# Another order of the eight groups of score products on TensorE's array tiles

## The chip, the cores and the metric

The kernel runs on one core of one Trainium2 chip. The metric is device time in microseconds of one execution. The engines are TensorE (PE, with its weight loads listed apart as PEld), VectorE (DVE), ScalarE (ACT), GpSimd (POOL) and SyncE (SP), which here issues nearly all DMAs. Each engine runs its own list of instructions in the order in which the program gives them, and engines wait for each other through semaphores.

## The reference

A cross-attention block with a feed-forward part, in float32: 128 sequences of 128 tokens, width 256, 16 heads of 16, hidden width 1024.

```python
q = (query @ Wq + bq).reshape(b, s, N_HEADS, D_K).transpose(0, 2, 1, 3)
k = (key @ Wk + bk).reshape(b, s, N_HEADS, D_K).transpose(0, 2, 1, 3)
v = (values @ Wv + bv).reshape(b, s, N_HEADS, D_K).transpose(0, 2, 1, 3)
scores = jnp.einsum('bhqd,bhkd->bhqk', q, k) / jnp.sqrt(jnp.float32(D_K))
allowed = j < i + mask
scores = jnp.where(allowed, scores, NEG_INF)
attn = jax.nn.softmax(scores, axis=-1)
...
ctx = ctx.transpose(0, 2, 1, 3).reshape(b, s, d)
attn_out = ctx @ Wo + bo
x = layer_norm(query + attn_out, ln1_g, ln1_b)
ffn = jax.nn.relu(x @ W1 + b1) @ W2 + b2
out = layer_norm(x + ffn, ln2_g, ln2_b)
```

With mask 0 a token attends only to the tokens before it, so the first 64 queries need only the first 64 keys.

## The kernel before

The 128 sequences are worked on as 64 pairs, numbered 0 to 63. Weights stay in SBUF. The kernel is a software pipeline written out by hand: in the regular step of pair p (pairs 9 to 60, `step`, a loop over the list `ORDER`) PE computes the scores and values of pair p, the queries and keys of p+1, the output projection of p-2, the first feed-forward product of p-4 or p-3 and the second of p-5 or p-4, and so on. The same operations stand one by one in a long list for the pairs ahead of 9 and behind 60. Nothing is reordered by a scheduler: each engine gets its instructions as the list names them, and the framework adds the semaphore waits.

PSUM is one tile, `banks`, of eight banks, which the operations share by hand. The change concerns `scores_both` (its matmul is L440), which is called for every pair from 4 on, in the regular step between `context` and `res0`:

- The queries qT and keys kT lie in SBUF with 32 rows for a group of heads, so there are four **strips** of 32 rows, r = 0 to 3. The 128x128 array of PE is used as eight tiles of 32 rows and 64 columns: the strip r gives the rows, the sequence s of the pair (0 or 1) the columns.
- Each strip has products for two values of m, and for two halves of the queries: `hi` = 0 is the first 64 queries, a **narrow** product of 128 columns, and `hi` = 1 the second 64 queries, a **wide** product of 256 columns. That gives 4 x 2 x 2 x 2 = 32 products, each left in the profile as two records.
- A wide product of strip r goes to bank r, a narrow one to bank 4 + r.
- `scores_both` issues them as eight groups of four: the strips 0 and 1 (`one`) or 2 and 3 (`two`), one half, one m, and in each group s outside and r inside.

Around it, within one step: `weigh` (L586, L596) multiplies the probabilities of pair p-2 with its values into bank 7, and DVE reads that bank in `context` (L612, then L617 twice). ACT reads banks 0 and 1 in `relu_even` (L1399, called re1 to re3). After the scores PE goes on with `v1`, the first value products (L1147). DVE then masks the narrow scores (L464 for banks 4 and 5, L456 for banks 6 and 7) and the wide ones (L1552, bank by bank, beginning with bank 3, then 1, 2 and 0, the last three behind `low_maximum`, L920). The keys reach kT through a DMA (`ks`, `ks2`, "kT<-kr"). `turnx` (L1614) is a transpose on DVE ahead of `context`.

```python
        weigh addbo re0-2 vr-1 hf-2 re2-2 re1-2 turnx-1 xc2-1 re3-2 context scores res0 ro3-2
        ro0-2 br1 maskA0 ro2-2 add3 oc0 ro1-2 v1 maskA1 oc2 maskB hs0-1 o1 max3 vk1 vk0 q1
```

Of the kernel before, what the change touches and what calls it, by code (L numbers as in the profile page):

```python
# [19 lines left out]
def tile_cross_attention_block(  # L20
# [165 lines left out]
    one = const.tile([1, P], F32, tag="one", name="one")  # L186
# [61 lines left out]
    def at_bank(i, name):  # L248
        return banks[:, i]
# [141 lines left out]
    def room(p, hi):  # L391

        st = states[p]
        if "sm" not in st:
            st["sm"] = wide(f"sm_{p}") if p != 1 else turned_all
        at = H * P if not hi else 0
        n = P if hi else HP
        st["sm", hi] = st["sm"][:, at : at + H * n].rearrange("p (h j) -> p h j", j=n)
        st["nmx", hi] = small.tile([P, H], F32, tag=f"nmx{hi}", name=f"nmx{hi}_{p}")
# [22 lines left out]
    def scores_both(p):  # L422

        st = states[p]
        st["both"] = True
        for hi in range(2):
            st["sps", hi] = [
                at_bank(r if hi else 4 + r, f"pss{hi}_{p}_{r}") for r in range(NS)
            ]
            room(p, hi)  # L430
        one, two = (0, 1), (2, 3)
        for strips, hi, m in (
            (one, 0, 0), (two, 1, 0), (one, 0, 1), (two, 1, 1),
            (one, 1, 0), (one, 1, 1), (two, 0, 0), (two, 0, 1),
        ):
            n = P if hi else HP
            for s in range(2):
                for r in strips:
                    strip, first = slice(32 * r, 32 * r + 32), s * P
                    nc.tensor.matmul(  # L440
                        st["sps", hi][r][
                            s * HP : (s + 1) * HP, m * 2 * n : (m + 1) * 2 * n
                        ].rearrange("p (e j) -> p e j", e=2),
                        st["qT"][strip, m, first + hi * HP : first + hi * HP + HP],
                        st["kT"][strip, m, :, first : first + n],
                        start=True, stop=True,
                    )
# [1190 lines left out]
    def bring_part(p, n):  # L1638
# [3 lines left out]
    OPS = {  # L1642
        "weigh": lambda p: weigh(p - 2),
        "scores": lambda p: scores_both(p),
        "context": lambda p: context(p - 2),
        "deviations": lambda p: scales_of(p),
# [381 lines left out]
    tokens(5, "c")  # L2028
    bring(3, nc.sync, LATE_FIRST[7:])
    scores_both(4)  # L2030
    mask(4, 0, A)
    mask(4, 1, A)
# [31 lines left out]
    spread_values(4)  # L2064
    stack_values(4)
    scores_both(5)
    tokens(6, "c")
    mask_high(5, 2, 2)
# [1024 lines left out]
```

## Time and profile before

| What | us |
|---|---|
| median of three runs | 1478.88 |
| lowest and highest run | 1476.47, 1479.12 |
| span of the profiled execution, first to last instruction | 1476.0 |
| PE busy in it | 1450.0 |
| one regular step (pair 33 to pair 34) | 22.03 |
| score products, L440, of pair 33, from the first to the first product behind them | 1.60 |

No time of the profiled execution other than its span is listed, so the span stands for it, 0.47 us below the lowest run. In the rows of the profile a timeline entry gives start, duration, engine, line, operation and the tiles written and read, and how many instructions were merged; the duration of merged PE rows runs to the modelled end of the last one, so successive rows overlap. Rows of windows give the stretch, its length, and the busy time of each engine with the number of its instructions that ran in it: PE first, then PEld; the rows of a quarter to a tenth of a microsecond and shorter are restricted to L440.

### The profile page before, as it was taken

The numbers are of one execution on the slowest core, as the hardware profiler recorded it, in microseconds if no ns is written. First come the engines' busy times: TensorE is split into PE (matmuls) and PEld (weight loads), VectorE is DVE, ScalarE is ACT, GpSimd is POOL, SyncE is SP. The second block draws the span as 40 slices with busy tenths as digits, with TensorE's granted clock in tenths as the row PEclk, the third lists the DMA queues.
The fourth block names the chain that finished last, engine by engine and source line by source line (L and its number), as shares of the span: only waits on it lengthen the run. The fifth ranks groups of instructions, "written<-read, shape, count | busy, mean of one in ns | idle before, by whom it ended". The sixth has DMA issues, their size and how long they took to land.

```text
span 1476.0 us, 61938 instructions
## 1 busy us (share of the span) xinstructions
PE 1450.0 (98%) x20713; PEld 1394.3 (94%) x20713; DVE 1372.8 (93%) x3231; ACT 1304.3 (88%) x5559; POOL 1266.4 (86%) x1816
## 2 busy tenths in 40 slices
PE   8999899999999999999999999999999999999998
PEld 7778799999999999999999999999999999999988
DVE  6987999999999999999999999999999999999767
ACT  4659899999999999999999999999999999999743
POOL 5986898988988988988988988888898888887966
PEclk9999999999999999999999999999999999999999
DMA  8274766766766767776766766766776766774541
GB/s 202 66 142 104 178 162 149 159 152 156 167 158 155 154 152 157 169 159 152 165 147 151 166 157 157 163 149 153 163 160 157 161 147 154 163 163 113 130 109 51
DMA packets 367448, 220.33 MB, mean 149 GB/s; under 512 B 279600, under 2 KB 335152, under 8 KB 367152
## 3 DMA queue, kind: packets, MB, share of 16 engines
q1 hardware_dynamic: 364864, 214.27, 63.9%
q8 instruction: 187, 3.06, 0.9%
q10 hardware_dynamic: 2288, 2.11, 0.7%
q14 instruction: 109, 0.89, 0.2%
HBM read 55.06 MB, written 18.09 MB: 50 GB/s over the span
## 4 chain that ended last, share of the span: by engine, by line
PE 72%; ACT 7%; DVE 4%; DMA 3%; SPq 1%; POOL 1%; issue 1%; DVEq 0%; ACTq 0%; POOLq 0%
PE banks L1147 40%; PE banks L1358 20%; PE banks L440 5%; ACT sm L931 5%; PE banks L596 3%; DMA kT<-kr 2%; PE banks L586 2%; PE banks L971 1%; DMA brought<-turned 1%; ACT kr L1213 1%; PE banks L869 0%; PE banks L1044 0%; ACT qT L1175 0%; SPq L552 0%; PE banks L629 0%
## 5 line engine op out<-in xcount | busy, mean ns | idle before, releaser
L931 ACT ACTIVATE sm<-banks,nmx 128x128 f32<-128x128 f32 x944 | 336.8, 383 | 15.8 <-DVE nmx L1558 12.6
L931 ACT ACTIVATE sm<-sm,nmx 128x64 f32<-128x64 f32 x944 | 321.6, 369 | 1.4 <-DVE nmx L920 1.4
L533 DVE STREAM_TRANSPOSE turned<-sm 128x1024 f32<-128x1024 f32 x186 | 217.0, 1213 | 3.3 <-DMA brought<-turned 2.4
L931 ACT ACTIVATION_READ_ACCUMULATOR sm<-banks,nmx 128x1 f32 x944 | 211.4, 224 | 0.0
L931 ACT ACTIVATION_READ_ACCUMULATOR sm<-sm,nmx 128x1 f32 x944 | 207.8, 220 | 0.0
L1147 PE MATMUL banks<-wt,hS 128*128 128x128 f32 x1344 | 177.6, 275 | 0.0
L1358 PE MATMUL banks<-xS,w1t 128*128 128x128 f32 x1344 | 177.2, 275 | 0.0
L1147 PEld LDWEIGHTS banks<-wt,hS 128*128 128x128 f32 x1344 | 163.6, 192 | 0.1
L1358 PEld LDWEIGHTS banks<-xS,w1t 128*128 128x128 f32 x1344 | 163.4, 192 | 0.0
L1558 DVE TENSOR_REDUCE nmx<-banks 128x4 f32<-128x512 f32 x224 | 152.1, 679 | 1.9
L1547 POOL TENSOR_TENSOR hS<-hT 128x512 f32<-128x512 f32 x116 | 147.5, 1273 | 5.4 <-ACT hT L876 2.4
L1358 PE MATMUL banks<-brought,w 128*128 128x128 f32 x896 | 118.2, 275 | 0.0
L1608 POOL TENSOR_TENSOR x1b<-x,g_r 128x512 f32<-128x512 f32 x56 | 72.3, 1291 | 51.0 <-ACT x L703 51.0
L1147 PE MATMUL banks<-w,hT 128*128 128x128 f32 x896 | 109.8, 275 | 0.0
L1358 PEld LDWEIGHTS banks<-brought,w 128*128 128x128 f32 x896 | 109.0, 192 | 0.0
L440 PE MATMUL banks<-kT,qT 32*64 32x128 f32 (+1 forms) x3840 | 100.7, 331 | 6.3 <-DMA kT<-kr 3.7
L1147 PEld LDWEIGHTS banks<-w,hT 128*128 128x128 f32 x896 | 104.8, 192 | 0.1
L440 PEld LDWEIGHTS banks<-kT,qT 32*64 32x64 f32 x3840 | 82.7, 131 | 16.9 <-ACT hT L1399 4.9
L1534 POOL TENSOR_TENSOR oc<-cxT 128x128 f32<-128x128 f32 x112 | 49.0, 457 | 57.9 <-DVE cxT L617 56.9
L1387 ACT ACTIVATE hT<-hT,b1e_c 128x256 f32<-128x256 f32 x224 | 95.7, 509 | 1.2 <-DVE hT L1383 1.1
L1552 DVE TENSOR_TENSOR banks<-banks,neg 128x256 f32<-128x256 f32 x224 | 93.1, 416 | 0.0
L703 ACT ACTIVATE x<-t,nb,sd 128x256 f32<-128x256 f32 x126 | 68.4, 592 | 19.1 <-POOL nb L726 11.9
(322 smaller groups left out, 4841.1 us busy)
## 6 DMA issues: line engine op xcount, KB each, us to landing
brought<-turned SPq DMA_DIRECT2D x936, 128.0 KB, 2.4
out_dram<-t SPq DMA_DIRECT2D x63, 256.0 KB, 4.7
xb<-in_x_dram SPq DMA_DIRECT2D x124, 128.0 KB, 3.2
cb<-in_ctx_dram SPq DMA_DIRECT2D x124, 128.0 KB, 3.2
x<-in_x_dram SPq DMA_DIRECT2D x31, 512.0 KB, 5.4
kT<-kr SPq DMA_DIRECT2D x112, 128.0 KB, 2.7
brought<-turned SPq DMA_DIRECT2D x40, 96.0 KB, 2.2
w<-in_L_xattn_W_dram SPq DMA_DIRECT2D x2, 1024.0 KB, 7.8
```

Of the source, the lines that this page charges most:

```text
L440: nc.tensor.matmul(st["sps", hi][r][s * HP : (s + 1) * HP, m * 2 * n : (m + 1) * 2 * n].rearrange("p (e j) -> p e j", e=2), st["qT"][strip ...
L533: nc.vector.transpose(turned[:, :, at : at + 256].rearrange("p j (n a) -> p n j a", a=32), states[p]["sm", hi].rearrange("p h j -> p (h j) ...
L703: nc.scalar.activation(x1[:, s], t1[:, s], AF.Identity, bias=st["nb", 1][:, s], scale=sd[:, s])
L931: nc.scalar.activation(sm[:, h, :], src, AF.Exp, bias=nmx[:, h : h + 1], scale=1.0, **({"accum_out": st["su"][:, at : at + 1]} if summed e ...
L1147: nc.tensor.matmul(out, left(k) if self.depth > 1 else left, right(k) if self.depth > 1 else right, start=(n == 1 and k == 0), stop=(k == ...
L1358: nc.tensor.matmul(ps[:, i * P : (i + 1) * P].rearrange("p (n a) -> p n a", a=32), left(i), right, start=(n in (1, 2, 5) and i == 0), stop ...
L1387: nc.scalar.activation(self.hT[:, f, at], self.hT[:, f, at] if src is None else src, AF.Relu, bias=b1e_c[:, f : f + 1], scale=1.0,)
L1534: nc.gpsimd.tensor_tensor(c[:, n], left, right, how)
L1547: engine.tensor_tensor(c[:, n], left, right, how)
L1552: nc.vector.tensor_tensor(ps[:, :, HP:], ps[:, :, HP:], neg[:, 1, None, :].to_broadcast([P, 4, HP]), ALU.add)
L1558: nc.vector.tensor_reduce(states[p]["nmx", 1][:, 4 * b : 4 * b + 4], banks[:, b].rearrange("p (n j) -> p n j", j=P), AX.X, ALU.max, negate ...
L1608: nc.gpsimd.tensor_tensor(st["x1b"], st["x1b"] if n else st["x1"], (be1b_r if n else g1_r)[:, None, :].to_broadcast([P, 2, D]), ALU.add if ...
```

## The change

Of the eight groups in `scores_both`, two change places with the next one. The fourth group, the wide one of strips 2 and 3 with m = 1, goes behind the wide one of strips 0 and 1 with m = 0. The wide one of strips 0 and 1 with m = 1 goes behind the narrow one of strips 2 and 3 with m = 0.

```diff
         for strips, hi, m in (
-            (one, 0, 0), (two, 1, 0), (one, 0, 1), (two, 1, 1),
-            (one, 1, 0), (one, 1, 1), (two, 0, 0), (two, 0, 1),
+            (one, 0, 0), (two, 1, 0), (one, 0, 1), (one, 1, 0),
+            (two, 1, 1), (two, 0, 0), (one, 1, 1), (two, 0, 1),
         ):
```

On each strip the order of its own products is the same as before: narrow, narrow, wide, wide on strips 0 and 1, and wide, wide, narrow, narrow on strips 2 and 3. The first place is PE in pair 10, from the end of `weigh` to `v1`, before the change. The size is that of the output: 64x128 is a narrow product, 64x256 a wide one; kT and qT are the keys and queries of this pair.

```order
L596 MATMUL banks<-brought,vz_174 32x64 x16
L440 MATMUL banks<-kT_170,qT_3025 64x128 [waits DMAHW5_49,DMAHW4_49,Activation_49]
L440 MATMUL banks<-kT_170,qT_3025 64x128 x3
L440 MATMUL banks<-kT_170,qT_3025 64x256 [waits DVE_49]
L440 MATMUL banks<-kT_170,qT_3025 64x256 x3
L440 MATMUL banks<-kT_170,qT_3025 64x128 x4
L440 MATMUL banks<-kT_170,qT_3025 64x256 x4
L440 MATMUL banks<-kT_170,qT_3025 64x256 [waits Activation_49]
L440 MATMUL banks<-kT_170,qT_3025 64x256 x7
L440 MATMUL banks<-kT_170,qT_3025 64x128
L440 MATMUL banks<-kT_170,qT_3025 64x128 [waits DVE_49]
L440 MATMUL banks<-kT_170,qT_3025 64x128 x6
```

And the same place after the change:

```order
L440 MATMUL banks<-kT_170,qT_3025 64x256 [waits DVE_49]
L440 MATMUL banks<-kT_170,qT_3025 64x256 x3
L440 MATMUL banks<-kT_170,qT_3025 64x128 x4
L440 MATMUL banks<-kT_170,qT_3025 64x256 [waits Activation_49]
L440 MATMUL banks<-kT_170,qT_3025 64x256 x7
L440 MATMUL banks<-kT_170,qT_3025 64x128
L440 MATMUL banks<-kT_170,qT_3025 64x128 [waits DVE_49]
L440 MATMUL banks<-kT_170,qT_3025 64x128 x2
L440 MATMUL banks<-kT_170,qT_3025 64x256 x4
L440 MATMUL banks<-kT_170,qT_3025 64x128 x4
L1147 MATMUL banks<-wv,cT_3063 128x128 [waits DVE_49]
```

The product that waits for ACT, into bank 0, was the 17th of the 32 and is the 13th. The second narrow product of strips 2 and 3, into bank 7, which waits for DVE, was the 26th and is the 22nd; four wide products of strips 0 and 1 that stood ahead of it stand behind it now.

The second place is PE in pair 6, one of the pairs ahead of the regular step, before the change. Here the third group, narrow on strips 0 and 1, waits for ACT in its first product:

```order
L440 MATMUL banks<-kT_170,qT_1648 64x128 [waits Activation_49]
L440 MATMUL banks<-kT_170,qT_1648 64x128 [waits DVE_49]
L440 MATMUL banks<-kT_170,qT_1648 64x128 x2
L440 MATMUL banks<-kT_170,qT_1648 64x256 x4
L440 MATMUL banks<-kT_170,qT_1648 64x128 [waits Activation_49]
L440 MATMUL banks<-kT_170,qT_1648 64x128 x3
L440 MATMUL banks<-kT_170,qT_1648 64x256 x5
L440 MATMUL banks<-kT_170,qT_1648 64x256 [waits Activation_49]
L440 MATMUL banks<-kT_170,qT_1648 64x256 x6
```

Behind the waiting narrow group stand, before the change, four wide products of strips 2 and 3 without a wait of their own; after it the wide group of strips 0 and 1 takes that place. DVE, ACT, POOL and SP have the same rows before and after.

## The prediction

> **What bounds the kernel now.** I read the page first: its busy shares and its chain of waits.
>
> ```profile
> span 1476.0 us, 61938 instructions
> PE 1450.0 (98%) x20713; PEld 1394.3 (94%) x20713; DVE 1372.8 (93%) x3231; ACT 1304.3 (88%) x5559; POOL 1266.4 (86%) x1816
> PEclk9999999999999999999999999999999999999999
> PE 72%; ACT 7%; DVE 4%; DMA 3%; SPq 1%; POOL 1%; issue 1%; DVEq 0%; ACTq 0%; POOLq 0%
> PE banks L1147 40%; PE banks L1358 20%; PE banks L440 5%; ACT sm L931 5%; PE banks L596 3%; DMA kT<-kr 2%; PE banks L586 2%; PE banks L971 1%; DMA brought<-turned 1%; ACT kr L1213 1%; PE banks L869 0%; PE banks L1044 0%; ACT qT L1175 0%; SPq L552 0%; PE banks L629 0%
> ```
>
> PE is busy for 98% of the span at full granted clock, and the chain that ended last runs mostly over PE; the score products, L440, hold 5% of it. A nanosecond that PE gains or loses inside the score stage is therefore a nanosecond of the step, unless PE then waits for something else. So I went to the timeline of PE at pair 33 and at its neighbours, and to the busy sums of that step.
>
> ```profile
> 717.62:739.65 22.03, 22.03 (x335) 21.59 (x328) 21.30 (x53) 20.90 (x93) 19.60 (x29) 1.00 0.73 170
> 717.62 1.67 PE L440 MATMUL banks<-kT,qT 32*64 32x128 f32 x64
> 719.22 0.71 PE L1147 MATMUL banks<-wv,cT 128*128 128x128 f32 x4
> 739.65 1.67 PE L440 MATMUL banks<-kT,qT 32*64 32x128 f32 x64
> 695.67 1.59 PE L440 MATMUL banks<-kT,qT 32*64 32x128 f32 x64 [0.21 <-ACT hT L1399]
> 697.19 0.71 PE L1147 MATMUL banks<-wv,cT 128*128 128x128 f32 x4
> ```
>
> The first row gives a whole step from one score stage to the next: 22.03 us, with PE (its first number) busy for all of it. The score stage of pair 33 starts at 717.62 and the next products start at 719.22: 1.60 us. Its 32 products leave 64 records, so each goes through the array in two passes. Pair 32 reached its stage late, after a wait of 0.21 us, and took 697.19 - 695.67 = 1.52 us from its first record. The two kinds differ, so something inside the stage binds when PE comes on time. The rows of DVE beside it show what is still running:
>
> ```profile
> 717.76 0.42 DVE L612 TENSOR_TENSOR cxT<-banks,brought 128x256 f32<-128x256 f32 x1
> 718.10 0.47 DVE L617 TENSOR_TENSOR cxT<-banks,brought 128x124 f32<-128x124 f32 x2
> 718.50 0.42 DVE L464 TENSOR_TENSOR sm<-banks,neg 128x256 f32<-128x256 f32 x1
> 718.84 0.42 DVE L1552 TENSOR_TENSOR banks<-banks,neg 128x256 f32<-128x256 f32 x1
> 720.70 1.21 DVE L920 TENSOR_REDUCE nmx<-sm 128x16 f32<-128x1024 f32 x1
> ```
>
> And these are the narrow passes under way in two short windows, first from 718.605 to 718.63, then from 718.63 to 718.66:
>
> ```profile
> L440 PE MATMUL banks<-kT,qT 32*64 32x128 f32 x1 | 0.3, 268 | 0.0
> ...
> L440 PE MATMUL banks<-kT,qT 32*64 32x128 f32 x4 | 0.4, 306 | 0.0
> ```
>
> The narrow products (128 columns, the low half) of strips 2 and 3 write banks 6 and 7. Bank 7 also holds the context of pair 31, which DVE reads in `context` (L612, L617) until 718.10 + 0.47 = 718.57. Just before 718.63 one narrow pass runs, the one into bank 6; from 718.63 there are four. So the second product of this group waits for DVE and starts 0.06 us after L617 ends, and the third and fourth, which have no wait of their own, start with it: what stands behind a waiting product is held too. From that release the stage takes 719.22 - 718.63 = **0.59 us** more. I call the release R.
>
> **The change, part by part.** It adds and removes nothing: the same 32 products, the same waits, and DVE, ACT, POOL and SP have identical rows. On PE two groups change places with a neighbour.
>
> First: the wide group of strips 0 and 1, m=0, moves ahead of the wide group of strips 2 and 3, m=1. It carries a wait for ACT (its bank must be read out by the ReLU, L1399). That wait now also holds the group behind it.
>
> ```profile
> 716.68 1.20 ACT L1399 ACTIVATE hT<-banks,b1e_c 128x256 f32<-128x256 f32 x3 [0.16 <-DVE hT L1397]
> 717.91:717.95 0.04, 0.04 (x20) 0.04 (x12) 1.00 0.00 0
> ```
>
> L1399 ends at 716.68 + 1.20 = 717.88; with the 0.06 us that R needed after its releaser the wait is over at 717.94. The group behind it has weights that load as soon as their strips start the second pass before (12 loads are active around 717.93), but its array tiles stream the first wide group until about 718.1, two passes of 0.216 us (below) from the stage's start. So I cost the held loads at nothing; the cover is the running pass. If it were gone the price would be what L1399 is late. The gain of this first exchange is that these wide products no longer come 17th to 20th. At present three of the four loads come late:
>
> ```profile
> 718.07:718.08 0.01, 0.01 (x16) 0.01 (x1) 1.00 0.00 0
> 718.12:718.13 0.01, 0.01 (x15) 0.01 (x5) 1.00 0.00 0
> ```
>
> The second number pair is weight loads under way: only one at 718.07, five by 718.12. Three of the newcomers are the missing loads of this group, up to 0.08 us after the first, which had to start with its strips' last narrow pass. The strips lose up to 0.04 us by it. That is not on the path that ends the stage in a step like pair 33, because strips 2 and 3 end it, through R. In a late pair, where R is early, it may be: there I bound the first exchange by 0 and by -0.04 us a pair.
>
> Second: the narrow group of strips 2 and 3, m=0, with the wait for DVE in its second product, moves **ahead of the wide group of strips 0 and 1, m=1**. This is the term that counts. Today those four wide products pass before the wait and stream while PE is held; strips 0 and 1 finish with strips 2 and 3. After the change they stand behind the waiting product. Their strips fall idle, and at R seven products are loaded in a row: three narrow, then four wide. That a wait holds products of the other strips as well, and how fast the held ones follow, can be read at pair 6, where a narrow product of strips 0 and 1 waits for ACT with the wide group of strips 2 and 3 behind it:
>
> ```profile
> 126.22:126.31 0.09, 0.09 (x16) 0.00 (x0) 1.00 0.42 91
> 126.31:126.35 0.04, 0.04 (x17) 0.03 (x4) 1.00 0.48 102
> 126.35:126.40 0.05, 0.05 (x16) 0.05 (x12) 1.00 1.93 410
> 717.62:717.64 0.03, 0.02 (x3) 0.02 (x4) 1.00 0.00 0
> 717.62:717.67 0.05, 0.05 (x8) 0.05 (x8) 1.00 0.00 0
> ```
>
> Here 126.27 is the same place in the stage as 717.91, where loads were running; at pair 6 none is (x0), though nothing but the waiting product stands in their way. Then twelve loads are active within 0.09 us. The last two rows give the pace: eight loads in 0.05 us, so 0.0066 us each.
>
> Now the sum for one step with R where pair 33 has it. The length of a pass comes from plain streams of PE:
>
> ```profile
> 713.15 1.06 PE L1358 MATMUL banks<-brought,w 128*128 128x128 f32 x8
> 714.04 1.06 PE L1358 MATMUL banks<-xS,w 128*128 128x128 f32 x8
> 38.28 1.89 PE L629 MATMUL banks<-wo,cxT 128*128 128x256 f32 x8
> 40.01 1.89 PE L356 MATMUL banks<-wv,cT 128*128 128x256 f32 x8
> ```
>
> A pass of 128 columns takes 0.89 / 8 = 0.111 us, one of 256 columns 1.73 / 8 = 0.216 us. Before, the last narrow product loaded at R needs four narrow passes (its own two and the two of m=1): 4 x 0.111 = 0.445 us, the remainder of the 0.59 being load, drain and the next load. After, the last wide product is loaded four places later, 4 x 0.0066 = 0.026 us, and needs two wide passes, 2 x 0.216 = 0.432 us. The stage ends 0.026 + 0.432 - 0.445 = 0.013 us later; if narrow passes are half a wide one (0.108) it is 0.026 us. I take **+0.02 us** a step, near the middle. The end cannot be earlier than before: the three narrow products still start at R, with the same four passes to go.
>
> How many steps:
>
> ```profile
> 231.94 1.67 PE L440 MATMUL banks<-kT,qT 32*64 32x128 f32 x64
> ...
> 1337.04 1.67 PE L440 MATMUL banks<-kT,qT 32*64 32x128 f32 x64
> ...
> 186.72 1.90 PE L440 MATMUL banks<-kT,qT 32*64 32x128 f32 x64
> 209.99 1.59 PE L440 MATMUL banks<-kT,qT 32*64 32x128 f32 x64 [0.94 <-DMA kT<-kr]
> ...
> 1359.07 1.74 PE L440 MATMUL banks<-kT,qT 32*64 32x128 f32 x64
> ```
>
> From the first of these rows, pair 11, to the second, pair 61, stand 51 pairs; 40 of them read 1.66 or 1.67 as these do, and 11 read 1.59 or 1.60, like pair 32. The 40 give 40 x 0.02 = **+0.8 us**. For pairs 9 and 62 (1.90 and 1.74), which hang on later releases in the same place, I add 0.04. The 11 late ones lie between 0 and 11 x -0.04 = -0.4 us; I take -0.1, near their nearest row, since their last loads, the narrow ones of m=1, stand where they stood. The other seven (4 to 8, 10 and 63) begin late or wait for other engines inside the stage; at 0.08 us each, the lateness of a load, they are worth -0.6 to +0.6, taken as 0.
>
> Nothing downstream absorbs or adds to this. DVE's masks (718.50, 718.84) each start as the one before ends, not on PE, and the mask at 718.84 reads strips 2 and 3, whose wide groups end by about 718.6 either way. The group that ends later now, the wide one of strips 0 and 1, is masked behind the reduction at 720.70, so after 721.9. The longer idle time of strips 0 and 1 costs nothing by itself.
>
> Sum: +0.8 + 0.04 - 0.1 = +0.7 us on a span of 1476.0, so 1476.7. No time of that execution beside its span is listed; the runs lie at 1476.47 to 1479.12, 0.5 to 3.1 us above the span. I add the change to their median: 1478.9 + 0.7 = **1479.6 us**.
>
> **The rivals.** A: *loads of the other strips pass the waiting product.* Then the wide loads do not stand behind it, the stage ends through R as before, and the late pairs can only gain: 0 to -0.4 us, 1478.5 to 1478.9. Against it: pair 6's row with no load at all. [...]
>
> B, the other side: *only part of the held products is at hand at R.* If PE took in the wide products only as held ones leave, their loads would come 0.08 us later, as the three late loads did at 718.08. That decides from the moment fewer than seven products fit behind a wait: 0.08 + 0.02 = 0.10 us a step, 42 steps, +4.2 us: 1483.1. Against it: the twelve loads of pair 6 within 0.09 us, which are those of eight products and their next passes. For it: the late loads themselves, whose reason the trace does not show.
>
> C: *the new order gains in the stage by itself*, as an order that follows the tiles should: at best every on-time pair falls to the 1.52 us of pair 32, 40 x -0.08 = -3.2 us, 1475.7. It needs the wait for L617 to end earlier, and L617 hangs on DVE rows that do not move. That the change does nothing at all is excluded by the order itself; that it does nothing measurable is my forecast.
>
> **How the numbers follow.** Forecast 0.74, A 0.11, B 0.11, C 0.04. About 0.2%, 3 us, is what a measurement of this kernel can tell from no change; the three runs shown differ by 2.7 us. Forecast and A lie within it, B lies beyond it on the slow side, C on the fast one; for scatter I move 0.01 to each side. Slower 0.12, same 0.83, faster 0.05. The range runs from the forecast less the distance of the lowest run from the median (2.4) and the late pairs' 0.4, 1476.8, up to B, 1483.2.
>
> **What would show it.** In the profile of the changed kernel, pair 33's stage should read 1.62 us where it read 1.60, L617 should end at the same place in it, and just before R no wide pass of m=1 should run for strips 0 and 1: the count of wide passes at R falls from twelve to those still draining. Right after R seven loads should follow each other within 0.05 us. A would show wide passes before R and 1.60; B 1.70 with a gap in the loads. I would be wrong if late pairs became more or fewer: one wait for kT before a stage can be worth 0.94 us, as at 209.99, more than the whole forecast.

## The result and the profile after

| | before | after |
|---|---|---|
| median, us (22 runs each, on the same chip) | 1475.78 | 1480.12 |
| lowest and highest, us | 1471.22, 1479.27 | 1472.63, 1485.65 |
| ratio after / before | | 1.0024 (95% interval 1.0013 to 1.0034) |
| span of the profiled execution, us | 1476.0 | 1479.9 |
| mean granted clock of PE in it | 0.997 | 0.995 |

The changed kernel is slower by 0.24%, 1475.78 x 0.0024 = 3.5 us (interval 1.9 to 5.0; the medians lie 4.3 apart), where +0.7 us was forecast. That the predicted time fits is luck: its median of 1480.12 lies near the predicted 1479.6 only because the forecast stood on three runs of the kernel before with a median of 1478.88, 3.1 us above the 1475.78 that it has beside the changed kernel.

The page of the changed kernel, busy shares and the first line of the chain:

```profile
span 1479.9 us, 61938 instructions
PE 1453.0 (98%) x20713; PEld 1391.3 (94%) x20713; DVE 1374.5 (93%) x3231; ACT 1304.4 (88%) x5559; POOL 1266.7 (86%) x1816
PE 81%; ACT 6%; DVE 5%; DMA 3%; POOL 2%; SPq 1%; issue 1%; DVEq 0%; POOLq 0%; ACTq 0%
```

PE gained 3.0 us of busy time (1450.0 to 1453.0) with the same 20713 instructions: some of its products took longer. First comes the step that the forecast was about, pair 33 and its late neighbour, in the timeline of PE and DVE (start, duration, engine, line, operation, tiles):

```profile
699.77 1.56 PE L440 MATMUL banks<-kT,qT 32*64 32x128 f32 x64 [0.94 <-DMA kT<-kr]
701.26 0.71 PE L1147 MATMUL banks<-wv,cT 128*128 128x128 f32 x4
721.69 1.70 PE L440 MATMUL banks<-kT,qT 32*64 32x128 f32 x64
722.17 0.48 DVE L617 TENSOR_TENSOR cxT<-banks,brought 128x124 f32<-128x124 f32 x2
723.32 0.71 PE L1147 MATMUL banks<-wv,cT 128*128 128x128 f32 x4
```

The on-time stage now takes 723.32 - 721.69 = 1.63 us (1.60 before), the late one 701.26 - 699.77 = 1.49 us from its first record (1.52 before). L617 ends at 722.65, 0.96 us behind the stage's start, against 718.57 - 717.62 = 0.95 us: R has not moved. The windows around R, restricted to L440, and then the same products by form, from 718.605 to 718.63 before the change and from 722.66 to 722.69 in the changed kernel:

```profile
722.65:722.69 0.04, 0.04 (x9) 0.04 (x1) 1.00 0.00 0
722.70:722.75 0.05, 0.05 (x16) 0.05 (x7) 1.00 0.00 0
```

```profile
L440 PE MATMUL banks<-kT,qT x13: 268/374/374, 718.3 to 718.6; 32*64 32x256 f32 x12, 32*64 32x128 f32 x1
L440 PE MATMUL banks<-kT,qT x9: 268/374/374, 722.4 to 722.6; 32*64 32x256 f32 x8, 32*64 32x128 f32 x1
```

Just before R eight wide passes still drain beside one narrow one, where twelve ran before; behind R seven loads come within 0.05 us. That is the mechanism that the forecast gave the second exchange, in all its parts. From pair 11 to pair 61 the profiled executions take 1340.58 - 234.51 = 1106.07 us, before 1105.10: +0.97. One execution of each can't show so small a sum, though: e2_pair5 below, with the order of before in all these pairs, took 1102.56 us. The length of the stages is what tells; it is the same within 0.01 us in nearly all on-time stages of an execution.

Most of the loss lies elsewhere, and comparing the starts of the score stages pair by pair finds it at pair 5, in the start-up. The kernel before, timelines of PE, DVE and ACT:

```profile
106.47 1.12 PE L440 MATMUL banks<-kT,qT 32*64 32x128 f32 x34
107.75 0.70 DVE L911 TENSOR_TENSOR banks<-banks,neg 128x512 f32<-128x512 f32 x1 [0.24 <-PE banks L440]
107.91 1.09 PE L440 MATMUL banks<-kT,qT 32*64 32x256 f32 x30 [0.32 <-ACT vd L379]
110.09 1.99 PE L300 MATMUL banks<-xT,wq 128*128 128x256 f32 x8 [1.10 <-DVE sm L464]
111.92 1.89 PE L629 MATMUL banks<-wo,cxT 128*128 128x256 f32 x8
125.98 2.22 PE L440 MATMUL banks<-kT,qT 32*64 32x128 f32 x64
126.06 0.82 ACT L379 COPY vd<-banks 64x256 f32<-64x256 f32 x2
128.13 1.99 PE L629 MATMUL banks<-wo,cxT 128*128 128x256 f32 x8
```

and the changed kernel:

```profile
107.26 1.08 PE L440 MATMUL banks<-kT,qT 32*64 32x128 f32 x26
108.70 1.12 PE L440 MATMUL banks<-kT,qT 32*64 32x256 f32 x38 [0.36 <-ACT vd L379]
109.57 0.70 DVE L911 TENSOR_TENSOR banks<-banks,neg 128x512 f32<-128x512 f32 x1 [1.33 <-PE banks L440]
111.92 2.40 PE L300 MATMUL banks<-xT,wq 128*128 128x256 f32 x8 [2.10 <-DVE sm L464]
114.11 3.21 PE L629 MATMUL banks<-wo,cxT 128*128 128x256 f32 x8
128.52 0.76 ACT L379 COPY vd<-banks 64x256 f32<-64x256 f32 x2
129.29 1.57 PE L440 MATMUL banks<-kT,qT 32*64 32x128 f32 x64
130.97 1.56 PE L629 MATMUL banks<-wo,cxT 128*128 128x256 f32 x6
```

At pair 5 the wide group of strips 0 and 1, m=0, waits for ACT (`stack_values`, L379) in the middle of the stage. Before, 34 records ran ahead of that wait, now 26: the wide group of strips 2 and 3, m=1, has fallen behind it by the first exchange. The first thing that DVE does after this stage is `mask_high` (L911) on banks 2 and 3, the banks of those strips. It now starts 2.31 us after the stage's start instead of 1.28, and everything behind it on DVE shifts: L464 frees a bank for the query products L300, and PE's pause there grows **from 1.10 to 2.10 us**.

Then a second thing happens. L629, eight passes in each kernel, lasts 1.89 us before and 3.21 us after. Windows of two microseconds show why; the last three columns are the granted clock, the DMA share and GB/s. Before, then after:

```profile
112.00:114.00 2.00, 2.00 (x11) 1.77 (x10) 1.93 (x5) 2.00 (x14) 0.00 (x0) 1.00 0.61 145
```

```profile
113.00:115.00 2.00, 2.00 (x8) 1.60 (x7) 1.97 (x3) 2.00 (x14) 0.00 (x0) 0.59 0.67 159
115.00:117.00 2.00, 2.00 (x7) 1.61 (x6) 1.14 (x3) 2.00 (x14) 0.00 (x0) 0.55 0.42 99
```

In windows of half a microsecond the granted clock of the changed kernel reads 1.00 until 113.0, 0.87 from 113.0 to 113.5, 0.50 in each of the six from 113.5 to 116.5, 0.72 from 116.5 to 117.0 and 1.00 behind it: (0.13 + 6 x 0.50 + 0.28) x 0.5 / 0.5 = 3.41 us at half clock. From the start of pair 5's stage to the end of pair 6's (the start of L629) the kernel before takes 128.13 - 106.47 = 21.66 us, the changed one 130.97 - 107.26 = 23.71. The 3.9 us between the two spans are: 0.79 ahead of pair 5 (a half-clock stretch more in the first 25 us, 6.83 us at half clock instead of 3.41; 0.03 of it the longer stage of pair 4), **2.05 in pairs 5 and 6**, and 1.06 behind them. Only the middle term is steady: over the fourteen profiled executions of this case pair 5's stage begins anywhere from 103.26 to 107.26 us, and the kernels before and after differ only from pair 4 on, at 88 us, so the first 25 us are not the change's doing.

### The profile page after: what moved, and what is told of

Its sections match the earlier page's. It is cut to its first block, busy times and chain, and to the rows that moved or that the text cites. A ratio compares the mean times of both kernels' runs of the same rounds, so it can differ in the third digit from the quotient of the medians.

```text
span 1479.9 us, 61938 instructions
## 1 busy us (share of the span) xinstructions
PE 1453.0 (98%) x20713; PEld 1391.3 (94%) x20713; DVE 1374.5 (93%) x3231; ACT 1304.4 (88%) x5559; POOL 1266.7 (86%) x1816
## 4 chain that ended last, share of the span: by engine, by line
PE 81%; ACT 6%; DVE 5%; DMA 3%; POOL 2%; SPq 1%; issue 1%; DVEq 0%; POOLq 0%; ACTq 0%
PE banks L1147 42%; PE banks L1358 21%; PE banks L440 6%; ACT sm L931 4%; PE banks L596 3%; PE banks L586 2%; PE banks L300 2%; PE banks L869 2%; DMA kT<-kr 2%; DMA brought<-turned 1%; PE banks L971 1%; PE banks L629 1%; SPq L552 1%; DVE sm L464 1%; PE banks L356 1%
## 5 line engine op out<-in xcount | busy, mean ns | idle before, releaser
L440 PE MATMUL banks<-kT,qT 32*64 32x128 f32 (+1 forms) x3840 | 101.1, 332 | 6.1 <-DMA kT<-kr 3.8
L440 PEld LDWEIGHTS banks<-kT,qT 32*64 32x64 f32 x3840 | 77.5, 131 | 21.3 <-ACT hT L1399 5.4
```

The costliest lines, as they stand in the source:

```text
L440: nc.tensor.matmul(st["sps", hi][r][s * HP : (s + 1) * HP, m * 2 * n : (m + 1) * 2 * n].rearrange("p (e j) -> p e j", e=2), st["qT"][strip ...
```

## The experiments

All ratios are to the kernel before on the same chip. "First" and "second" are the two exchanges of the prediction; the groups are (strips, half, m), and `...` stands for what is unchanged.

**Which pairs, and which exchange.** The first two kernels use the new order for some pairs only; NEW and OLD stand here for the two lists of groups.

```diff
-        for strips, hi, m in (NEW):
+        for strips, hi, m in NEW if p > 8 else OLD:      # e1_from9
+        for strips, hi, m in NEW if p == 5 else OLD:     # e2_pair5
```

> The new order stands in pairs 9 to 63 only; pairs 4 to 8 keep the order of before. Theory T (two places): the regular steps give 40 x +0.027 - 11 x 0.032 = +0.7 us, and the rest of the +3.5 us comes from pair 5, where the wide group of strips 2 and 3 now stands behind a wait for ACT. T expects the score stages as in the changed kernel (1.62 us on time, 1.52 us late), pair 5 as before (mask L911 1.28 us after the stage starts) and +0.7 us in all, ratio 1.000 to 1.001. Rival U (the steps alone): pair 5 is chance, ratio 1.002.

> The new order stands in pair 5 alone. Theory T: L911 starts 2.3 us after the stage instead of 1.28, the product behind the stage (L300) 4.66 us after it instead of 3.62, so +1.0 us, and +1.6 us more in runs where the pause of PE makes the granted clock fall; ratio 1.0007 to 1.0018; all other stages 1.60 and 1.55 us. Rival U: ratio 1.000.

e1_from9: 1475.82 us, ratio 1.0006 (0.9997 to 1.0015). e2_pair5: 1478.14 us, ratio 1.0018 (1.0006 to 1.0029). By the medians one of 64 pairs carries more than the 55 from pair 9 on; the two intervals overlap, so the exchanges are needed to part the two causes.

The next two apply one exchange each, to all pairs.

```diff
 # e3_first
-            (one, 0, 0), (two, 1, 0), (one, 0, 1), (two, 1, 1), (one, 1, 0), ...
+            (one, 0, 0), (two, 1, 0), (one, 0, 1), (one, 1, 0), (two, 1, 1), ...
 # e4_second
-            ... (one, 1, 0), (one, 1, 1), (two, 0, 0), (two, 0, 1),
+            ... (one, 1, 0), (two, 0, 0), (one, 1, 1), (two, 0, 1),
```

> In all pairs only the first exchange (wide m=0 of strips 0 and 1 ahead of wide m=1 of strips 2 and 3); wide m=1 of strips 0 and 1 stays ahead of the waiting narrow group. Theory T: on-time stages 1.60 us as before, late ones 1.52 us (-0.3 us in all), pair 5 as in the changed kernel (+1.0 us, +2.6 with the clock); ratio 1.0005 to 1.0016. Rival V (the second exchange makes all of it): ratio 0.9998, pair 5 as before.

> In all pairs only the second exchange (narrow m=0 of strips 2 and 3 ahead of wide m=1 of strips 0 and 1). Theory T: on-time stages 1.62 us, late ones 1.55 us, pair 5 as before (L911 at 1.28 us): +1.1 us, ratio 1.0007. Rival V: the whole +3.5 us, ratio 1.0024.

e3_first: 1477.62 us, ratio 1.0026 (1.0016 to 1.0037). e4_second: 1475.31 us, ratio 1.0005 (0.9996 to 1.0014). PE's timelines at pair 33, e3_first and then e4_second, and at pair 5 of e3_first:

```profile
717.80 1.67 PE L440 MATMUL banks<-kT,qT 32*64 32x128 f32 x64
719.40 0.71 PE L1147 MATMUL banks<-wv,cT 128*128 128x128 f32 x4
...
110.59 2.77 PE L300 MATMUL banks<-xT,wq 128*128 128x256 f32 x8 [2.10 <-DVE sm L464]
```

```profile
718.45 1.69 PE L440 MATMUL banks<-kT,qT 32*64 32x128 f32 x64
720.08 0.71 PE L1147 MATMUL banks<-wv,cT 128*128 128x128 f32 x4
```

The second exchange alone makes the on-time step 1.63 us and leaves pair 5 as it was; the first alone leaves the step at 1.60 us, shortens the late ones to 1.52 us from their first weight load (1.55 before; 1.49 and 1.52 from their first product), and has the pause of 2.10 us. The costly one is the exchange that the prediction priced at nothing.

The granted clock of every timed run tells the same. A stretch of 3.41 us at half clock lowers a run's mean by 3.41 / 2 / 1476 = 0.0012. Means over the runs of this comparison: kernel before 0.9972 (32 runs), e1_from9 0.9975, e4_second 0.9973, but e2_pair5 0.9957 and e3_first 0.9957. The changed kernel's 22 runs have 0.9958.

**Is it the pause that takes the clock?** One kernel makes PE pause at pair 5 in the old order, the other gives it work during the pause of the new order: the narrow products of strips 2 and 3, m=0, once more.

```diff
 # e5_pause: the old order
     scores_both(5)
+    empty(35)
 # e6_fill: the new order
     scores_both(5)
+    for _ in range(8):
+        for s in range(2):
+            for r in (2, 3):
+                nc.tensor.matmul(
+                    states[5]["sps", 0][r][s * HP : (s + 1) * HP, : 2 * HP].rearrange(
+                        "p (e j) -> p e j", e=2
+                    ),
+                    states[5]["qT"][32 * r : 32 * r + 32, 0, s * P : s * P + HP],
+                    states[5]["kT"][32 * r : 32 * r + 32, 0, :, s * P : s * P + HP],
+                    start=True, stop=True,
+                )
```

> The old order everywhere; behind pair 5's score stage PE gets 35 empty instructions, about 0.07 us each, so that its pause there grows from 1.10 us to about 2.1 us, as with the new order, and no other engine's work is moved. Theory K (a pause of PE of about 2 us in one piece halves the granted clock for 3.41 us soon after, whatever made it): the profile shows a half clock for 3.41 us within pairs 5 and 6, the mean granted clock of the runs falls from 0.997 to about 0.996, and the time rises by the pause (0.9 us) and by 1.7 us, +2.6 us, ratio about 1.0018. Rival L (the clock falls for another reason, the order of products or what DVE does): full clock in pairs 5 and 6, +0.9 us at most, ratio about 1.0006.

> The new order everywhere; behind pair 5's score stage four narrow products of strips 2 and 3 are repeated eight times, with the same result, so that PE has work for about 1.8 us of its pause of 2.1 us. L464 and the query products behind it should start where they do with the new order alone. Theory K (the pause takes the clock): full clock in pairs 5 and 6, mean granted clock of the runs back at 0.997; what is left is the wait, +1.0 us, and the 0.7 us of the later steps: +1.7 us, ratio about 1.0012, and one half-clock stretch less than the new order has. Rival L: half clock in pair 5 or 6 all the same, ratio 1.0024 as the new order has.

As times both missed far: e5_pause 1485.01 us, ratio 1.0075 (1.0057 to 1.0092), e6_fill 1532.26 us, ratio 1.0396 (1.0381 to 1.0410). Both lose it in the regular steps, hundreds of microseconds behind the edit; that is taken up below. The stretch in question can be read in the profiles all the same. PE's timeline of e6_fill at pairs 5 and 6, and a window of it:

```profile
103.73 1.08 PE L440 MATMUL banks<-kT,qT 32*64 32x128 f32 x26
106.11 1.93 PE L2070 MATMUL banks<-kT,qT 32*64 32x128 f32 x64
108.39 1.99 PE L300 MATMUL banks<-xT,wq 128*128 128x256 f32 x8 [0.35 <-DVE sm L464]
126.47 1.99 PE L629 MATMUL banks<-wo,cxT 128*128 128x256 f32 x8
```

```profile
110.00:112.00 2.00, 2.00 (x11) 1.76 (x10) 1.93 (x5) 2.00 (x13) 0.00 (x0) 1.00 0.63 151
```

L300 starts 108.39 - 103.73 = 4.66 us after the stage's start, as in the changed kernel, but PE has idled only 0.35 us, and the clock stays full, 1.00 in each window of half a microsecond from 104 to 127: 126.47 - 103.73 = 22.74 us to the end of pair 6's stage. In e5_pause the pause was 1.61 us, less than meant, and the clock was halved from 107.7 to 111.1:

```profile
107.88 3.58 PE L300 MATMUL banks<-xT,wq 128*128 128x256 f32 x8 [1.61 <-DVE sm L464]
```

The mean clock over the runs is 0.9979 for the kernel before (16 runs), 0.9973 for e6_fill (4) and 0.9963 for e5_pause (6). That is the expected order, but four runs can't say whether e6_fill is free of the half clock every time.

**What the insertions did.** In e5_pause the program of all engines is that of the kernel before, apart from the 35 empty instructions; still pairs 11 to 61 took 1344.20 - 230.11 = 1114.09 us instead of 1105.10, while the executions without an insertion lie between 1102.56 and 1106.55. In e6_fill PE stops in the score stage of the regular step, with no engine named that it waited for:

```profile
741.20 1.13 PE L440 MATMUL banks<-kT,qT 32*64 32x256 f32 x40 [0.74 <-issue]
```

So the place of PE's instructions in its own program might count, or their number. Two kernels change both and leave pair 5 alone:

```diff
 # e10_shift: 35 empty instructions more, among the first products
-        empty(2)    # behind each of eight products
+        empty(6)
-    empty(4)
+    empty(7)
 # e11_back: 36 fewer, between the key and query products of pair 0
-            empty(5)    # four times
+            empty(0)
-            empty(5)    # four times
+            empty(1)
```

> The old order; 35 empty instructions more on PE in its first 7 us, among the first products, where PE's queue is ahead of its array by more than they take. Theory S (where PE's instructions lie sets how PE gets them, and e5_pause lost 9 us in pairs 11 to 61 because everything behind its insertion lay 35 places later): the regular steps take about 22.18 us as in e5_pause, pairs 11 to 61 about 1114 us instead of 1105, ratio 1.005 or more. Rival (e5_pause lost them by what the pause at pair 5 did to the other engines): regular steps of 22.03 us, ratio 1.000.

> The old order; 36 empty instructions fewer on PE, taken from between the key and query products of pair 0 at 8 to 12 us, which take longer than they. Theory S: pairs 11 to 61 take another time than 1105 us, likely longer, with idle time of PE that no engine ends, at one place of each step. Rival: 1105 us, as before the change.

e10_shift: ratio 1.0048 (1.0034 to 1.0063), 1483.74 us; e11_back: one run of 1487.08 us. PE's timeline of e10_shift at pairs 11 and 61, and of e11_back in the regular step:

```profile
230.14 1.67 PE L440 MATMUL banks<-kT,qT 32*64 32x128 f32 x64
...
1343.61 1.67 PE L440 MATMUL banks<-kT,qT 32*64 32x128 f32 x64
```

```profile
696.61 0.54 PE L596 MATMUL banks<-brought,vz 128*32 128x64 f32 x22 [0.54 <-issue]
```

1113.47 us for pairs 11 to 61 of e10_shift, as in e5_pause; in e11_back PE stops inside `weigh`. Empty instructions of the first 12 us change the steps hundreds of microseconds later: 35 more or 36 fewer, and pairs 11 to 61 take 1113.47 or 1114.33 us instead of 1105.10. The last kernel undoes the shift and keeps the pause:

```diff
 # e12_moved: the old order; 42 empty instructions of pair 0 stand behind pair 5's stage
-    empty(4)
+    empty(2)
-            empty(5)    # eight times
+            empty(0)
     scores_both(5)
+    empty(42)
```

> The old order; 42 of PE's empty instructions are taken from among the products of pair 0 and put behind pair 5's score stage, so that from there on PE's instructions lie where they lay before the change, and PE's pause at pair 5 grows, by e5_pause's profile (35 of them made 0.49 us) to about 2.1 us, +1.0 us. Theory S: regular steps of 22.03 us, pairs 11 to 61 about 1105 us, without the 9 us of e5_pause and e10_shift. Theory K: half clock for 3.41 us at pair 5, the mean granted clock of the runs lower than that of the kernel before by about 0.001, and the time up by the pause and about 1.0 to 1.5 us of clock: +2.0 to +2.5 us, ratio 1.0014 to 1.0017. If the pause costs no clock: ratio 1.0007 at most.

e12_moved: 1476.32 us, ratio 1.0004 (0.9993 to 1.0016). Its timeline of PE and a window:

```profile
103.26 1.12 PE L440 MATMUL banks<-kT,qT 32*64 32x128 f32 x34
107.89 3.49 PE L300 MATMUL banks<-xT,wq 128*128 128x256 f32 x8 [2.10 <-DVE sm L456]
126.92 1.56 PE L629 MATMUL banks<-wo,cxT 128*128 128x256 f32 x6
230.87 1.67 PE L440 MATMUL banks<-kT,qT 32*64 32x128 f32 x64
...
1335.68 1.67 PE L440 MATMUL banks<-kT,qT 32*64 32x128 f32 x64
```

```profile
108.00:110.00 2.00, 2.00 (x6) 1.61 (x7) 1.97 (x3) 2.00 (x14) 0.00 (x0) 0.54 0.68 165
```

Pairs 11 to 61 take 1104.81 us: with the count of instructions restored, the 9 us are gone. The pause is 2.10 us, the clock is halved at once, and pairs 5 and 6 take 126.92 - 103.26 = 23.66 us, as in the changed kernel, with the old order and DVE undisturbed (L911 1.29 us after the stage's start). In this execution a pause is enough.

Over its runs, though, the price came out smaller than expected: the mean clock is 0.9968 beside 0.9972 for the kernel before, which 12 and 17 runs hardly tell apart, and the ratio's interval only just reaches the expected 1.0014. The edit may have won something back that the expectation left out: pair 4's stage begins at 84.08 us in e12_moved and at 84.14 in e11_back, the two kernels with empty instructions taken out of pair 0, and at 84.41 to 88.05 in the other twelve executions. Two executions don't show that this is the edit's doing.

**The regular step by itself, and better orders.** The diffs are to the new order; e8_first9 leaves the first exchange alone standing.

```diff
 # e7_split: all pairs; e9_split9: from pair 9 on, OLD below
-            (two, 1, 1), (two, 0, 0), (one, 1, 1), (two, 0, 1),
+            (two, 1, 1), ((2,), 0, 0), (one, 1, 1), ((3,), 0, 0), (two, 0, 1),
 # e8_first9: from pair 9 on, OLD below
-            (two, 1, 1), (two, 0, 0), (one, 1, 1), (two, 0, 1),
+            (two, 1, 1), (one, 1, 1), (two, 0, 0), (two, 0, 1),
```

> The new order, but of the narrow group of strips 2 and 3, m=0, only the half of strip 2 stands ahead of the wide group of strips 0 and 1, m=1; the half of strip 3, which waits for DVE at R, stands behind that wide group again. If the 0.02 us of a regular step come from the wide products held behind the waiting one, an on-time step takes 1.60 us as before the change, late ones 1.52 us. Rival: the place of the narrow products among the wide ones costs it by itself, and on-time steps take 1.62 us. Pair 5 as in the new order (4.66 us).

> Only the first exchange, and only from pair 9 on; pairs 4 to 8 keep the old order. Expected: on-time steps 1.60 us, late ones 1.52 us, pair 5 as before the change (3.63 us, PE's pause 1.10 us), so 0 to -0.4 us, ratio about 0.9998: not told apart from the kernel before. If the later steps carried any of the change's loss it would show here as over +0.7 us.

> The old order for pairs 4 to 8; from pair 9 on the order of e7_split: the first exchange, and of the narrow group of strips 2 and 3, m=0, the half of strip 2 ahead of the wide group of strips 0 and 1, m=1, the half of strip 3 behind it. By e7_split's profile an on-time step takes 1.59 us and a late one 1.52 us, against 1.60 and 1.55 before the change: 42 x -0.006 and 10 x -0.03, -0.5 us in all, and pair 5 stays as it was before the change. Expected ratio 0.9997, so at the edge of what can be told from no change; 1.0006 or more would say that the new order loses something in the later steps that the stage lengths do not show.

PE's timeline of e7_split, pair 33:

```profile
717.59 1.66 PE L440 MATMUL banks<-kT,qT 32*64 32x128 f32 x64
719.19 0.71 PE L1147 MATMUL banks<-wv,cT 128*128 128x128 f32 x4
```

1.60 us in these rounded starts, 1.59 by its nanoseconds: with the wide group of strips 0 and 1 no longer behind the product that waits for DVE, the 0.03 us are gone, and late steps keep their 1.52. The cost of the second exchange is the work held behind that product. e8_first9 has ratio 1.0001 (0.9992 to 1.0010), e9_split9 1.0000 (0.9988 to 1.0012). e7_split was run once, 1475.81 us, too little for a comparison of times. The two others cost nothing that can be measured; their stages gain at most half a microsecond in all, and nothing faster than the kernel before was found.

**The prices side by side.** From the start of pair 5's stage to the end of pair 6's, in the profiled executions:

| | PE idle at L300, us | half clock in pairs 5 and 6 | us |
|---|---|---|---|
| before, e1_from9, e4_second, e9_split9, e10_shift | 1.10 | no | 21.66 to 21.71 |
| e8_first9, e11_back (old order at pair 5) | 1.10 | yes | 22.68 |
| e6_fill (new order, PE given work) | 0.35 | no | 22.74 |
| e5_pause | 1.61 | yes | 23.09 |
| after, e2_pair5, e3_first, e7_split | 2.10 | yes | 23.50 to 23.72 |
| e12_moved | 2.10 | yes | 23.66 |

The later mask alone costs 22.74 - 21.66 = 1.08 us, the half clock alone 22.68 - 21.66 = 1.02; together that is 2.10, and the changed kernel shows 2.05. The half clock costs less than the 1.7 us by which its products grow, since in the kernel before pair 6's stage waits for ACT (it takes 128.13 - 125.98 = 2.15 us); in the changed kernel, 1.68 us, PE comes so late that L379 is just done (128.52 + 0.76 = 129.28, the stage begins at 129.29). The clock was halved in six of six executions with a pause of 1.6 us or more, in two of seven with 1.10, and not in the one with 0.35.

What parts the two from the five is where the pause fell. The half-clock stretches of one execution start whole multiples of 3.41 us apart, and in e8_first9 and e11_back the interval of 3.41 us ahead of the stretch held the wait for L379 (0.32 us) and the whole pause: PE was busy for 1.99 us of it. In the five others no such interval held so much idle time: the lowest is 2.14 us busy, in e10_shift, against 2.31 before; in e1_from9 and e4_second the pause lies in two intervals. In the six with the longer pause it was 1.31 to 1.62 us.

## Why the prediction was right and wrong

**The number: luck.** The predicted time fits by the offset of 3.1 us named above; the change itself was mis-sized, +0.7 us for +3.5.

**The second exchange: right.** R stayed where it was, the count of wide passes before R fell, seven loads followed R within 0.05 us, and the step lengthened as computed, by 0.027 us (1.597 to 1.624) where 0.02 was taken and 0.026 was the upper value of its two. 42 of the pairs 11 to 61 were on time, +1.1 us. e4_second and e7_split show that this exchange and the held products are its cause.

**The first exchange, late pairs: right, at the edge.** Each late stage took 0.03 us less; the bound was 0.04, the value taken 0.01. Nine pairs, -0.3 us. The sum for the steps was +0.7; the profiles give +0.97 for pairs 11 to 61, which also holds two late pairs fewer and lies within what single executions differ by, and e1_from9 has ratio 1.0006, +0.9 us, which its interval (0.9997 to 1.0015) does not tell from 0.

**The step that failed** is the sentence on the first exchange, "I cost the held loads at nothing; the cover is the running pass", together with "the other seven (4 to 8, 10 and 63) ... at 0.08 us each ... taken as 0". The cover was read at pair 33, where L1399 is ready within 0.32 us of the stage's start. At pair 5 the same product waits for another releaser, L379, which comes 0.36 us after the running passes have ended; there is no cover. The price of a gone cover was put at "what L1399 is late", which is PE's own loss. The real one runs over another engine: that DVE's masks "each start as the one before ends, not on PE" holds in the regular step, but at pair 5 DVE waits for PE, and waits for just the banks that the held group writes. The row that shows it was in the trace of before: L911, idle 0.24 us, ended by PE L440. Instead of 0 the term measured +1.08 us.

**The term that was missing** is the granted clock. A pause of PE of 2.10 us brought a half clock of 3.41 us, worth another 1.0 us in the profile. No rival had it. Rival A is excluded by the windows at R, B by the seven loads in 0.05 us, and C by the on-time stages. The chance of 0.12 for a time slower by more than about 0.2% was carried by B; what came was slower by about that much for another reason.

**What stays open.** The terms add up to about 1.1 (the mask) + 1.0 (the half clock) + 0.9 (the other steps, by e1_from9) = 3.0 us, inside the measured interval of 1.9 to 5.0 us for the changed kernel, but e3_first has no cost in the on-time steps and still measured 1.0026, and e12_moved with the same 2 us in its profile measured 1.0004. How often the pause really takes the clock, and what else those runs lost, the profiles, one execution each, do not say. The difference of 0.0014 in mean clock is 1.2 stretches per run, one of which was seen. Half-clock stretches also come and go elsewhere: six of the fourteen profiled executions have one that starts between 158 and 162 us, old orders and new, and the first 25 us hold none, one or two. Why 35 instructions more or 36 fewer on PE cost 8 to 9 us in the regular steps was not found either, nor whether their position or their number does it; only that the loss goes when both are restored.

## What to carry to other kernels

A reorder that puts a waiting product ahead of others has to be priced at every place where the list is used, the start-up too, and for each held group the question is who reads its bank next, and whether that reader waits. A pause of PE costs its length and then perhaps its clock: here a pause of 1.10 us had a half clock with it in two of seven executions, one of 1.61 or 2.10 us in six of six. So look at the granted clock behind a pause that grows, and at what other idle time lies close to it. And compare orders that leave the count of an engine's instructions alone; an insertion, even of empty instructions, can move the time by more than what it was meant to test (the 35 of e5_pause cost 9.0 us in pairs 11 to 61, where +2.6 us in all was expected).

## What the runs showed of the hardware

- **Half clock at a pause of 1.1 to 2.1 us.** By windows of half a microsecond, each stretch that ended inside a span of the fourteen executions lasted 3.41 us or twice that. At pair 5 it began, in the changed kernel, about 1.4 us after the pause had ended (113.37 against 111.92), in e12_moved 0.3 us after, in e2_pair5 0.4 us before (108.72 against 109.12), and the starts within one execution lie whole multiples of 3.41 us apart (28 and 414 in the changed kernel, counted from its first), so in these executions they follow a grid of their own rather than the pause. A pause of 2.10 us was enough in five of five executions, one of 1.61 us in e5_pause, and one of 1.10 us with a wait of 0.32 us in the same interval in e8_first9 and e11_back. At pair 5 the clock was halved behind every interval in which PE was busy for 1.99 us or less, and behind none with 2.14 or more. That is no general limit: in the kernel before, the interval from 159.75 to 163.16 us has PE busy for 1.67 us, and the clock behind it stayed full (1.00 from 163.16 to 166.57).
- **How many instructions PE has, or where they lie.** 35 empty instructions more in the first 7 us (e10_shift): pairs 11 to 61 take 1113.47 us instead of 1105.10. 36 fewer (e11_back): 1114.33 us, and PE stops in twelve of these steps for up to 1.09 us with no engine named. 42 moved from pair 0 to pair 5, with the count as before behind them (e12_moved): 1104.81 us.
- **A waiting product holds the other strips.** At pair 33 of the changed kernel four wide products of strips 0 and 1 stand behind a waiting one of strips 2 and 3; none was loaded before it, and all within 0.05 us of its release (x7 from 722.70 to 722.75). At pair 6 before, it is the other way round: no load for 0.09 us (x0 from 126.22 to 126.31) while a product of strips 0 and 1 waits ahead of those of strips 2 and 3.
